# Half of image 0's convolution units placed among the attention slots of image 1

## The chip, the cores and the metric

The kernel runs on one core of a Trainium2 chip. The metric is the device time of one execution in microseconds (us). Three runs of the kernel before the change gave 2925.95, 2923.47 and 2923.46 us, median 2923.47 us.

## What is computed

The input x has 2 images of 256 channels and 64 x 64 pixels, all in float32. Two layers follow each other.

```python
# layer 0: attention over all 4096 pixels, 8 heads of 32, then a 1x1 convolution and a mask
q = proj(Wq, bq) / sqrt(32); k = proj(Wk, bk); v = proj(Wv, bv)
attn = softmax(einsum('bnd,bmd->bnm', q, k))
fuse = einsum('bnm,bmd->bnd', attn, v)
x = conv1x1(concat([x, fuse]), Wf, bf) * m + x * (1 - m)
# layer 1: channel gate, attention in 8x8 windows (4 heads of 64), shuffle, grouped convolutions
x = x * sigmoid(relu(xp @ ca_w1 + ca_b1) @ ca_w2 + ca_b2)
x = x + window_attention(x)
x = x.reshape(b, 4, 64, h, w).transpose(0, 2, 1, 3, 4).reshape(b, c, h, w)
y = relu(bn1(conv7x7(x, sa_w1, groups=64)))          # 4 channels in, 1 out per group
y = bn2(conv7x7(y, sa_w2, groups=64))                # 1 in, 4 out per group
return x * sigmoid(y)
```

## The kernel before the change

A prologue computes q, k and v of both images and writes them to DRAM. Then follows the function `pipeline`, in three stretches.

**Slots.** The attention of layer 0 is 1024 slots `(b, c, g, m)`: image b, chunk c of 512 query pixels (8 per image), group g of 4 heads (2), block m of 128 keys (32). One chunk is 64 slots. A slot has the matmuls of `scores` (L633, tile `sa`, array cut into pieces of 32 rows by 64 columns), three `Exp` activations from PSUM on ACT (L646, tile `ea`), the matmuls of `products` (L669, tile `ava`, pieces of 128 rows by 32 columns) and an addition of 128x2048 on DVE (L675). Scores are issued two slots ahead of products. The PSUM banks of the scores come from two pools: three single banks, of which a slot takes two, and two pairs, of which it takes one. They are handed out in turn, so a bank is free again when ACT has read what stood in it.

**Stages.** What follows the attention of a chunk is the generator `stage`: the 1x1 convolution (`hya`), the channel gate (`ca1a`, `ca2a`), the window attention (`qka`, `sca`, `vwa`, `pta`, `oa`) and the output projection (`opa`). One step of it is issued after every fourth slot of the next chunk. Its last step writes the rows of layer 1's x to the DRAM tensor `xs` (L989) for the convolutions. The generator `bands` fills the convolutions' banded weights in DRAM (`ws`), one DMA after every fifth slot.

**Convolutions.** The 64 groups are worked off in 16 units of 4 groups. A unit of an image is: weights `wa` (896 KB, L1029) and rows (420 KB, `xea` or `xla`, L1036) loaded over SP's queue; `conv1` (L1057, `c1a`, pieces of 128x32); a `Relu` on ACT (L1065); `conv2` (L1082, `c2a`, pieces of 32x64); two `Tanh` (L1093) and a `Copy` (L1099) on ACT; the gate on DVE (L1110); 12 stores to the output (L1128, L1130). All of it runs at the end. The generator `convolve` takes the items of the list below in turn; each of its steps issues `conv1` of item k+1 and then `conv2` of item k. The first eight items need only image 0's rows and are issued between the stages of the last chunk. From the ninth on, an item needs rows that the last stage writes. In this text an item is named by its number, from 0: `c1(8)` is `conv1` of the ninth item.

```python
items = [(u, (0,)) for u in range(EARLY)] + [(u, (1,)) for u in range(2, EARLY)]
items += [(u, (0, 1)) for u in range(EARLY, NU)] + [(1, (1,)), (0, (1,))]
```

So items 0 to 13 are units of one image, items 14 to 21 work on both images at once, and items 22 and 23 are of one image again. Each engine runs its instructions in program order. Stores that are to go over ACT's queue are kept in `held` and issued after the next item's `conv2`, behind ACT's work on it.

Of the kernel before, what the change touches and what calls it, by code (L numbers as in the profile page):

```python
# [10 lines left out]
F32 = mybir.dt.float32  # L11
# [8 lines left out]
P = 128  # L20
# [12 lines left out]
EARLY = 8  # L33
# [17 lines left out]
ROOM = 4 * len(BLOCKS) * UG * WP  # L51
# [6 lines left out]
def conv_seq_kernel(ctx: ExitStack, tc: tile.TileContext, a, out):  # L58
# [464 lines left out]
    def pipeline(arm, shifted, pools):  # L523
# [130 lines left out]
        def products(i):  # L654
            b, c, g, m = slots[i]
            chains = 1 if (b, c) == (B - 1, NCHUNK - 1) else 2
            if m == 0:
                acc[0] = avp.tile([P, CH], F32, tag="av", name=f"av{arm}_{i}")
                acc[1] = ep.tile([P, HG, CH], F32, tag="sum", name=f"sum{arm}_{i}", bufs=3)
                totals[b, c, g] = acc[1]  # L660
                if chains == 2:
                    room = cpool.tile([P, ROOM], F32, tag="room", name=f"odd{arm}_{i}")
                    acc[2] = room[:, 0 : HG * CH].rearrange("p (h n) -> p h n", h=HG)
# [67 lines left out]
        def stage(b, c):  # L731
# [241 lines left out]
            for oc in range(KC):  # L973
# [5 lines left out]
                for n, (x0, _, _) in enumerate(BLOCKS):  # L979
# [4 lines left out]
                    for h in range(2):  # L984
                        q = 2 * oc + h
                        p = 32 * q + 1 - x0

                        eng = nc.sync if h == 1 and (b, c) == (B - 1, NCHUNK - 1) else nc.gpsimd
                        eng.dma_start(  # L989
                            x_s[b, n, p + r0 : p + r1].rearrange("r g w -> g r w"),  # L990
                            xo[64 * h : 64 * h + 64, oc, r0 - WS * c : r1 - WS * c, :],
                        )
# [5 lines left out]
        items = [(u, (0,)) for u in range(EARLY)] + [(u, (1,)) for u in range(2, EARLY)]  # L998
        items += [(u, (0, 1)) for u in range(EARLY, NU)] + [(1, (1,)), (0, (1,))]
        staged, held = [], deque()  # L1000

        def convolve():
            nb = len(BLOCKS)


            early, xcs, ycs = [], [], []
            room = cpool.tile([P, ROOM], F32, tag="room", name=f"xe{arm}")
            room = room.rearrange("p (k n g w) -> p k n g w", k=4, n=nb, g=UG)
            for k in range(4):
                early.append(room[:, k])  # L1010
            for k in range(2):
                t = cpool.tile([P, B * nb, WP], F32, name=f"yc{arm}{k}")
                nc.gpsimd.memset(t, 0.0)
                ycs.append(t)
            xs, ws, ys = {}, {}, {}

            weights = deque([*range(1, NU), 1])
            dst = out.rearrange("b (g i) r w -> b i r g w", i=4)

            def load_w(u):  # L1020
                if u >= NU:
                    return
                n = 2 * 32 * UW
                if u == 0:
                    t = cpool.tile([P, n], F32, name=f"w{arm}{u}")
# [6 lines left out]
            def load_x(k):  # L1032
                u, images = items[k]
                x = xs[k] = early[k % 4] if k < EARLY else xcs[k % 4]
                for i, b in enumerate(images):
                    nc.sync.dma_start(  # L1036
                        x[:, nb * i : nb * i + nb].rearrange("p n g w -> p n (g w)"),
                        x_s[b, :, :, UG * u : UG * u + UG, :].rearrange("n p g w -> p n (g w)"),
                    )

            def load_rows(k):

                while len(xs) < min(k + 1, len(items)) and (
                    staged or B - 1 not in items[len(xs)][1]
                ):
                    load_x(len(xs))

            def conv1(k):
                if k >= len(items):
                    return  # L1050
                u, images = items[k]
                n = nb * len(images)
                w = ws[u][:, 0 : 32 * UW].rearrange("p (m g d) -> p g d m", g=UG, d=KS)
                s = psum1(f"c1{arm}{k}")
                for d in range(KS):
                    for j in range(4):
                        nc.tensor.matmul(  # L1057
                            s[32 * j : 32 * j + 32, 0 : n * W],
                            w[:, j, d, :],
                            xs[k][:, 0:n, j, d : d + W],  # L1060
                            start=(d == 0),
                            stop=(d == KS - 1),
                        )
                y = ys[k] = ycs[k % 2]
                nc.scalar.activation(  # L1065
                    y[:, 0:n, PAD : PAD + W],
                    s[:, 0 : n * W].rearrange("p (n x) -> p n x", x=W),
                    AF.Relu,
                    bias=cbias1[:, u : u + 1],
                )  # L1070

            def conv2(k):
                u, images = items[k]
                n = nb * len(images)
                y = ys.pop(k)
                w = ws[u][:, 32 * UW :].rearrange("p (m d) -> p d m", d=KS)
                tiles = [psum2(f"c2{arm}{k}_{hh}") for hh in range(2)]
                for d in range(KS):
                    for j in range(4):
                        r = slice(32 * j, 32 * j + 32)  # L1080
                        for o in HALVES:
                            nc.tensor.matmul(  # L1082
                                tiles[j // 2][o, j % 2, 0 : n * W],
                                w[r, d, o],
                                y[r, 0:n, d : d + W],
                                start=(d == 0),
                                stop=(d == KS - 1),
                            )
                zs = []
                for m in range(len(images)):  # L1090
                    z = pool.tile([P, 4, nb * W], F32, tag="z", name=f"z{arm}{k}_{m}", bufs=4)
                    for hh in range(2):
                        nc.scalar.activation(  # L1093
                            z[:, 2 * hh : 2 * hh + 2, :],
                            tiles[hh][:, :, m * nb * W : (m + 1) * nb * W],
                            AF.Tanh,
                            scale=0.5,
                        )
                    nc.scalar.activation(z, z, AF.Copy, bias=0.25, scale=0.25)  # L1099
                    zs.append(z.rearrange("p j (n x) -> p j n x", x=W))  # L1100
                while held:
                    held.popleft()()
                return zs

            def gate(k, zs):
                u, images = items[k]
                for m, b in enumerate(images):
                    z = zs[m]
                    x = xs[k][:, nb * m : nb * m + nb, :, PAD : PAD + W]
                    nc.vector.tensor_mul(z, z, x.rearrange("p n g x -> p g n x"))  # L1110

                    engines = (nc.gpsimd, nc.sync)
                    if k >= len(items) - 2:
                        engines = (nc.scalar, nc.sync)
                    elif staged and k < EARLY:
                        engines = (nc.gpsimd, nc.scalar)
                    stores = 0
                    for n, (x0, r0, r1) in enumerate(BLOCKS):
                        for i in range(4):
                            p = 32 * i + 1 - x0  # L1120
                            stores += 1
                            args = (
                                dst[b, i, r0:r1, UG * u : UG * u + UG, :],
                                z[p + r0 : p + r1, :, n, :],
                            )
                            eng = engines[stores % len(engines)]
                            if eng is nc.scalar:
                                held.append(lambda a=args: nc.scalar.dma_start(*a))  # L1128
                            else:
                                eng.dma_start(*args)  # L1130
                if k == len(items) - 1:
                    while held:
                        held.popleft()()


            def more():
                if staged and not xcs:

                    for n in range(3):
                        t = ep.tile([P, HG, CH], F32, tag="sum", name=f"xl{arm}{n}", bufs=3)  # L1140
                        t = t.rearrange("p h n -> p (h n)")[:, 0 : B * nb * UG * WP]
                        xcs.append(t.rearrange("p (n g w) -> p n g w", n=B * nb, g=UG, w=WP))
                    xcs.append(pool.tile([P, B * nb, UG, WP], F32, name=f"xl{arm}3"))
                    load_rows(EARLY + 3)
                return bool(xcs)


            load_rows(3)
            load_w(0)
            pool = yield  # L1150
            for _ in range(4):
                load_w(weights.popleft())
            conv1(0)
            yield
            for k, (u, images) in enumerate(items):
# [167 lines left out]
```

## Time and profile before

| what | value |
|---|---|
| median of three runs | 2923.47 us |
| the profiled execution | 2921.04 us |
| its span, first to last instruction | 2919.3 us |
| PE busy with matmuls | 2881.9 us, 99% of the span |
| ACT busy | 2455.9 us, 84% |
| DVE busy | 2434.9 us, 83% |
| POOL busy | 315.1 us, 11% |
| granted TensorE clock, mean | 0.996 |
| last product of the attention begins | about 2700.4 us |
| last matmul ends | about 2904.8 us |

The span is counted from the first instruction. PE is TensorE's matmuls, PEld its weight loads, ACT ScalarE, DVE VectorE, POOL GpSimd, SP the engine whose queue issues most DMAs. A row of a timeline gives the start, the duration of the merged group, the engine, the line of the kernel, the tile written and read, and the idle time of the engine before it with what ended it. The profiler records every matmul of the program as two instructions. The profiled execution is 2.4 us below the median of the runs; differences that are worked out from it are added to the median.

### The profile page before, as it was taken

The numbers are of one execution on the slowest core, as the hardware profiler recorded it, in microseconds if no ns is written. First come the engines' busy times: TensorE is split into PE (matmuls) and PEld (weight loads), VectorE is DVE, ScalarE is ACT, GpSimd is POOL, SyncE is SP. The second block draws the span as 40 slices with busy tenths as digits, with TensorE's granted clock in tenths as the row PEclk, the third lists the DMA queues.
The fourth block names the chain that finished last, engine by engine and source line by source line (L and its number), as shares of the span: only waits on it lengthen the run. The fifth ranks groups of instructions, "written<-read, shape, count | busy, mean of one in ns | idle before, by whom it ended". The sixth has DMA issues, their size and how long they took to land.

```text
span 2919.3 us, 85528 instructions
## 1 busy us (share of the span) xinstructions
PE 2881.9 (99%) x37322; PEld 837.2 (29%) x37322; DVE 2434.9 (83%) x1356; ACT 2455.9 (84%) x4143; POOL 315.1 (11%) x560
## 2 busy tenths in 40 slices
PE   9999999999999999999999999999999999999998
PEld 3551222222222222222222222222222222222665
DVE  3339999899999898998989999989899899999211
ACT  5569989898989898988989898989899898989433
POOL 8010000000000101010000000000101010000356
PEclk9999999999999999999999999999999999999999
DMA  8545422222232323242222223222324232232474
GB/s 245 202 172 174 134 75 63 78 68 80 56 88 65 90 61 91 65 80 71 70 75 69 79 55 82 64 83 63 77 73 84 70 73 75 69 113 88 117 228 120
DMA packets 231124, 276.26 MB, mean 95 GB/s; under 512 B 118672, under 2 KB 135252, under 8 KB 230484
## 3 DMA queue, kind: packets, MB, share of 16 engines
q1 hardware_dynamic: 200996, 231.74, 27.3%
q0 software_dynamic: 22416, 35.61, 5.5%
q8 instruction: 295, 4.83, 0.7%
q10 hardware_dynamic: 7328, 3.36, 0.4%
q14 instruction: 89, 0.73, 0.1%
HBM read 221.88 MB, written 66.39 MB: 99 GB/s over the span
## 4 chain that ended last, share of the span: by engine, by line
PE 97%; DMA 1%; ACT 1%; DVE 0%; issue 0%; SPq 0%; POOL 0%; ACTq 0%; DVEq 0%; POOLq 0%
PE sa L633 37%; PE ava L669 35%; PE hya L519 4%; PE qka L519 4%; PE c2a L1082 2%; PE q L428 2%; PE c1a L1057 2%; PE opa L519 2%; PE vwa L519 2%; PE v L465 2%; PE k L428 2%; PE dna L695 1%; PE sca L847 1%; PE pta L922 1%; PE oa L941 1%; PE ca2a L785 1%
## 5 line engine op out<-in xcount | busy, mean ns | idle before, releaser
L646 ACT ACTIVATE ea<-sa 128x512 f32<-128x512 f32 (+1 forms) x3072 | 2036.7, 746 | 51.6 <-PE sa L633 26.6
L633 PE MATMUL sa<-qa,ka 32*64 32x512 f32 x16384 | 1145.9, 613 | 1.5 <-ACT vst L473 1.2
L675 DVE TENSOR_TENSOR suma<-suma,ea 128x2048 f32<-128x2048 f32 x480 | 1097.4, 2286 | 5.7 <-ACT ea L646 0.5
L669 PE MATMUL ava<-ea,va 128*32 128x512 f32 x8192 | 1091.1, 605 | 1.0
L675 DVE TENSOR_TENSOR odda<-odda,ea 128x2048 f32<-128x2048 f32 x420 | 959.4, 2284 | 50.6 <-ACT ea L646 50.6
L633 PEld LDWEIGHTS sa<-qa,ka 32*64 32x64 f32 x16384 | 241.7, 129 | 785.4 <-ACT ea L646 713.6
L669 PEld LDWEIGHTS ava<-ea,va 128*32 128x32 f32 x8192 | 161.5, 108 | 834.1 <-issue 804.6
L989 POOL DMA_DIRECT2D xs<-xo x94 | 66.6, 716 | 1761.8 <-DVE xo L974 1758.8
L675 DVE TENSOR_TENSOR suma<-ea,ea 128x2048 f32<-128x2048 f32 x32 | 73.2, 2287 | 58.8 <-ACT ea L646 58.8
L519 PE MATMUL qka<-ua,qkv_w 128*32 128x512 f32 x1024 | 115.8, 592 | 0.3 <-DVE ua L803 0.3
L1130 POOL DMA_DIRECT2D out_dram<-za x180 | 101.3, 571 | 77.8 <-DVE za L1110 56.3
L447 DVE TENSOR_REDUCE top<-sq 128x512 f32<-128x2048 f32 x16 | 36.6, 2286 | 81.6 <-ACT sq L441 81.6
L750 ACT ACTIVATE ta<-hya,bf 128x512 f32<-128x512 f32 x32 | 20.2, 683 | 97.3 <-PE hya L519 91.3
L1110 DVE TENSOR_TENSOR za<-za,xla 128x768 f32<-128x768 f32 x24 | 23.0, 960 | 94.3 <-ACT za L1099 53.7
L707 POOL DMA_DIRECT2D invs<-inva x62 | 34.1, 558 | 599.2 <-DVE inva L721 438.9
L754 DVE TENSOR_TENSOR ta<-ta,mca 128x512 f32<-128x512 f32 x32 | 22.0, 688 | 77.4 <-ACT ta L750 77.4
L868 ACT ACTIVATE ewa<-ewa,mxwa 128x64 f32<-128x64 f32 x256 | 85.3, 346 | 1.5 <-DVE mxwa L859 1.5
L1082 PE MATMUL c2a<-yca,wa 32*64 32x192 f32 (+1 forms) x2688 | 83.7, 387 | 2.6 <-issue 2.3
L1093 ACT ACTIVATE za<-c2a 128x384 f32<-128x384 f32 x64 | 27.8, 486 | 57.9 <-PE c2a L1082 41.6
L826 ACT ACTIVATE qka<-qka,qkv_b 128x512 f32<-128x512 f32 x64 | 40.3, 681 | 40.8 <-PE qka L519 40.8
L1082 PEld LDWEIGHTS c2a<-yca,wa 32*64 32x64 f32 x2688 | 64.7, 192 | 22.0 <-issue 12.7
L677 DVE TENSOR_TENSOR suma<-suma,odda 128x2048 f32<-128x2048 f32 x30 | 68.8, 2292 | 1.0
(138 smaller groups left out, 1675.9 us busy)
## 6 DMA issues: line engine op xcount, KB each, us to landing
ka<-ks SPq DMA_DIRECT2D x256, 256.0 KB
va<-vs SPq DMA_DIRECT2D x256, 256.0 KB
wa<-ws SPq DMA_DIRECT2D x17, 896.0 KB
ws<-zeros SPq DMA_DIRECT2D x16, 896.0 KB
xs<-xo POOLq DMA_DIRECT2D x78, 140.0 KB, 6.0
xla<-xs SPq DMA_DIRECT2D x24, 420.0 KB
x<-in_x_dram SPq DMA_DIRECT2D x16, 512.0 KB
qs<-qst SPq DMA_DIRECT2D x16, 512.0 KB
```

What stands on the lines that cost most here:

```text
L428: nc.tensor.matmul(s[:, g, :], w[:, kc, g * P : (g + 1) * P], rhs, start=(kc == 0), stop=(kc == KC - 1),)
L465: nc.tensor.matmul(sv[:, m, :], xs0[i][:, kc, m * P : (m + 1) * P], wv[:, kc, :], start=(kc == 0), stop=(kc == KC - 1),)
L519: nc.tensor.matmul(out[o : o + 32], weights[:, o : o + 32], x, start=start, stop=stop)
L633: nc.tensor.matmul(heads[j][o], k[r, cols][:, o], q[r, g, :], start=True, stop=not shifted)
L646: nc.scalar.activation(e[:, h, :], tile, AF.Exp, scale=SCALE0)
L669: nc.tensor.matmul(av[r, :], v[:, m % PB, r], e[:, j, :], start=start, stop=stop)
L675: nc.vector.tensor_add(total, first.pop(m % chains, total), e)
L677: nc.vector.tensor_add(acc[1], acc[1], acc[2])
L868: nc.scalar.activation(e[:, n, :], e[:, n, :], AF.Exp, bias=mx[:, n : n + 1], accum_out=rs[:, n : n + 1],)
L989: eng.dma_start(x_s[b, n, p + r0 : p + r1].rearrange("r g w -> g r w"), xo[64 * h : 64 * h + 64, oc, r0 - WS * c : r1 - WS * c, :],)
L1082: nc.tensor.matmul(tiles[j // 2][o, j % 2, 0 : n * W], w[r, d, o], y[r, 0:n, d : d + W], start=(d == 0), stop=(d == KS - 1),)
L1130: eng.dma_start(*args)
```

## The change

Units 0 to 7 of image 0 leave the end. A new generator `quiet` works them off among the slots of image 1 from its chunk 1 on, one step after every eighth slot, so two units in a chunk and all eight in chunks 1 to 4. Its four steps are: load weights and rows; `conv1`; `conv2` with its activations; gate and stores (all 12 over POOL's queue). The rest, 24 items, are all of one image: units 8 to 15 of image 0, units 8 to 15 of image 1, units 0 to 7 of image 1, in this order. For it:

- `bands` takes a step after every third slot, so that the weights are in DRAM before the first quiet unit.
- Weights are loaded 24 times instead of 17; rows that the last stage writes are loaded one item at a time, up to six items ahead, into six buffers (four, for two images each, before).
- In the last stage the rows written to `xs` go over ACT's and SP's queues instead of POOL's and SP's.
- The last item is evicted, gated and stored in three blocks of columns; the last three items' stores go over ACT and SP.

```diff
-EARLY = 8
+QUIET = 8
...
-                        eng = nc.sync if h == 1 and (b, c) == (B - 1, NCHUNK - 1) else nc.gpsimd
+                        eng = nc.gpsimd
+                        if (b, c) == (B - 1, NCHUNK - 1):
+                            eng = (nc.scalar, nc.sync)[h]
...
-        items = [(u, (0,)) for u in range(EARLY)] + [(u, (1,)) for u in range(2, EARLY)]
-        items += [(u, (0, 1)) for u in range(EARLY, NU)] + [(1, (1,)), (0, (1,))]
+        items = [(u, 0) for u in range(QUIET, NU)] + [(u, 1) for u in range(QUIET, NU)]
+        items += [(u, 1) for u in range(QUIET)]
+        fill = NU - QUIET
...
+        def evict(z, parts, cols):
+            for tile, h in parts:
+                nc.scalar.activation(z[:, h, cols], tile, AF.Tanh, scale=0.5)
+            nc.scalar.activation(z[:, :, cols], z[:, :, cols], AF.Copy, bias=0.25, scale=0.25)
...
+        def quiet():
+            for u in range(QUIET):
+                w = cpool.tile([P, 2 * 32 * UW], F32, tag="w0", name=f"wq{arm}{u}")
+                nc.sync.dma_start(w, w_s[u])
+                x = rows_of(cpool.tile([P, XU], F32, tag="xq", name=f"xq{arm}{u}"))
+                load_rows_of(x, u, 0)
+                yield
+                conv1(f"q{arm}{u}", u, w, x, ycs[u % 2])
+                yield
+                one, pair = psum1(f"c2q{arm}{u}_0"), psum2(f"c2q{arm}{u}_1")
+                last = psum1(f"c2q{arm}{u}_2")
+                conv2(w, ycs[u % 2], (one, pair[:, 0, :], pair[:, 1, :], last))
+                z = cpool.tile([P, 4, nb * W], F32, tag="zq", name=f"zq{arm}{u}")
+                parts = ((one, 0), (pair, slice(1, 3)), (last, 3))
+                parts = [(t[..., 0 : nb * W], h) for t, h in parts]
+                evict(z, parts, slice(0, nb * W))
+                yield
+                gate(z, x, slice(0, nb))
+                for n in range(nb):
+                    store(u, 0, n, z, (nc.gpsimd,))
+                yield
...
             def more():
                 if staged and not xcs:
...
+                        xcs.extend(rows_of(t[:, XU * k : XU * k + XU]) for k in range(2))
+                if unit[0] + 3 < fill:
+                    load_rows(unit[0] + 3)
+                elif xcs:
+                    load_rows(min(len(xs), unit[0] + 5))
                 return bool(xcs)
...
+            def finish(k, z, out_of):
+                u, b = items[k]
+                if k == len(items) - 1:
+                    for n in range(nb):
+                        out_of(slice(W * n, W * n + W))
+                        gate(z, xs[k], slice(n, n + 1))
+                        store(u, b, n, z, (nc.sync, nc.scalar))
+                    flush()
+                    return
+                gate(z, xs[k], slice(0, nb))
+                engines = (nc.gpsimd, nc.sync)
+                if staged and k < fill:
+                    engines = (nc.gpsimd, nc.scalar)
+                elif k >= len(items) - 3:
+                    engines = (nc.scalar, nc.sync)
+                for n in range(nb):
+                    store(u, b, n, z, engines)
...
-            if i % 5 == 1:
+            if i % 3 == 1:
                 next(banded, None)
+            if i % 8 == 2 and b == B - 1 and c > 0:
+                next(hushed, None)
```

## The prediction

> **What bounds the kernel now.** First the page: who is busy, and what the chain that ended last is made of.
>
> ```profile
> PE   9999999999999999999999999999999999999998
> ...
> ACT  5569989898989898988989898989899898989433
> ...
> PE 97%; DMA 1%; ACT 1%; DVE 0%; issue 0%; SPq 0%; POOL 0%; ACTq 0%; DVEq 0%; POOLq 0%
> ```
>
> PE carries the chain, but ACT is nearly as full among the slots and half empty at the end. Whether a slot has room for a convolution is therefore read from PE's timeline, where a stage's block stands between slots:
>
> ```profile
> 1149.29 1.11 PE L633 MATMUL sa<-qa,ka 32*64 32x512 f32 x16
> ...
> 1151.22 3.62 PE L519 MATMUL hya<-xa,WfT 128*32 128x512 f32 x32
> 1154.66 3.62 PE L519 MATMUL hya<-fa,WfT 128*32 128x512 f32 x32
> 1158.20 1.11 PE L633 MATMUL sa<-qa,ka 32*64 32x512 f32 x16
> ...
> 1160.24 1.11 PE L633 MATMUL sa<-qa,ka 32*64 32x512 f32 x16
> ...
> 1164.32 1.11 PE L633 MATMUL sa<-qa,ka 32*64 32x512 f32 x16
> ...
> 1166.25 1.05 PE L519 MATMUL ca1a<-x1a,ca_w 128*32 128x256 f32 x16
> 1167.23 1.11 PE L633 MATMUL sa<-qa,ka 32*64 32x512 f32 x16
> ```
>
> Scores start every 2.04 us. With the block `hya` the interval is 8.91 us: all of the block's 6.87 us is added. ACT's timeline for the same moment:
>
> ```profile
> 1158.34 1.26 ACT L750 ACTIVATE ta<-hya,bf 128x512 f32<-128x512 f32 x2 [5.92 <-PE hya L519]
> 1159.49 7.95 ACT L646 ACTIVATE ea<-sa 128x512 f32<-128x512 f32 x12
> ```
>
> ACT sat idle for 5.92 us, so every score bank was free, and PE could have run ahead. It did not: the next interval is 2.04 again (1158.20 to 1160.24). So 2.04 us is PE's own pace. ACT needs 7.95 us for four slots, 1.99 us for one: it is just fast enough, with little to spare.
>
> Last, PE's timeline of the end, and under it one stretch of the end (length; busy time of PE, PEld, DVE, ACT, POOL; clock, DMA share, GB/s):
>
> ```profile
> 2772.76 3.76 PE L1082 MATMUL c2a<-yca,wa 32*64 32x192 f32 x107 [1.73 <-issue]
> 2780.61 4.26 PE L1057 MATMUL c1a<-xla,wa 128*32 128x192 f32 x56 [4.09 <-ACT yca L1065]
> 2784.80 2.64 PE L1082 MATMUL c2a<-yca,wa 32*64 32x192 f32 x112
> 2787.37 2.53 PE L1057 MATMUL c1a<-xla,wa 128*32 128x192 f32 x56
> 2789.83 2.64 PE L1082 MATMUL c2a<-yca,wa 32*64 32x192 f32 x112
> ```
>
> ```profile
> 2775.00:2780.00 5.00, 1.52 (x35) 0.88 (x20) 0.00 (x0) 0.00 (x0) 0.57 (x1) 0.50 1.07 359
> ```
>
> The convolutions too are PE-bound: 2.46 us from `c2a` to the next `c1a` ending (2787.37 to 2789.83), 2.57 us for `c2a` (2784.80 to 2787.37). Items of two images take 4.73 and 4.80 us (chain of waits, 2822.69 on). The one real hole is at 2771 to 2781, where item 8 waits for rows that the last stage writes; the clock falls to 0.50 in it.
>
> **Added among the slots.** Eight `conv1` and eight `conv2`. The end's price is 2.46 + 2.57 = 5.03 us a unit. From below: `ca1a`, in `conv1`'s array form and beside slots, adds 2.90 - 2.04 = 0.86 us (1164.32 to 1167.23) for 16 matmuls of 256 columns. Scaled, 56 of 192 columns give 0.86 x 56/16 x 192/256 = 2.25 us; the two-image items agree (4.73 - 2.46 = 2.27). `conv2` likewise is between 4.80 - 2.57 = 2.23 and 2.57. What lies between the ends is a change of array form. In the slots `conv1` follows products of its own form and `conv2` comes before scores of its own form, so I take 2.3 + 2.4 = 4.7 us, near the lower end; eight units: 37.6 us (36 to 40.3).
>
> ACT adds per unit a `Relu` of 0.42, two `Tanh` reads and a `Copy`, 1.73 us in the end's rows (0.87 for two `Tanh` reads, 0.85 the `Copy`; here three reads, hence some 0.1 more). While PE is in the block ACT would have idled, but the eviction can only begin when `conv2` is over, and queued behind it on ACT are the next slot's exponentials, for which PE's scores two slots on wait. The nearest row is a copy of `f` (0.59 us on ACT) followed by one of `ewa` (0.6 us, beside 0.62 us on PE): the score interval behind them is 2.32, a stall of 0.28 us. I take 0.4 us a unit, 3.2 in all (0, as behind `hya`, to 1.0 each). Together **+40.8 us** (36 to 48).
>
> At nothing: DVE's gate (0.96 us) and POOL's 12 stores (12 x 0.57 = 6.8 us), in steps at slots 26 and 58 of a chunk, away from the stage's own stores at slots 0 and 8. SP gets two loads (896 and 420 KB) every 32 slots; queued behind them are key and value loads, asked for eight slots (16 us) ahead. A weight load took 6.1 us in the busy end (chain of waits, 2798.39), so the cover holds; without it up to 6 us for each of eight loads. `bands` issues the same DMAs in three fifths of the time: during the 16 fills of `ws` the DMA share is some 0.45 over 10 us stretches, and it would be some 0.75; PE's intervals show no trace of these fills now. Zero, with 2 us kept for the range.
>
> A rule speaks for more room: the Trainium skill, Perfetto Trace Analysis, "Identifying the Most-Contended Engine", says that PE's matmul occupancy does not tell how near it is to its limit, and names weight loads' busy share (here 29%) instead. By it the slots would have room and only ACT's 2.2 us a unit would be paid, some 18 us instead of 40.8; the 2.04 us behind an idle ACT says that the room cannot be used by this order of instructions.
>
> **Taken from the end.** Up to `conv1` of item 8 the list has the same eight items of one image, so PE's order is the same there. From 2780.61 to the last matmul's end at 2904.80 were 124.2 us: eight `c1a` of one image (19.7), eight of two (37.8), nine `c2a` of one (23.1), eight of two (38.4), sum 119.0, and 5.2 of waits and slow clock (`c1a` at 2780.61 took 4.26 for 2.46). After: 16 x 2.46 + 17 x 2.57 = 83.1 us. Of the eight moved units, worth 40.2 us, 4.4 is given back, because 8 x 9.53 for pairs become 16 x 5.03. Waits after: slow clock 1.8 again, 0.3 before the last `conv2` (2902.43), and for the DMA 1.5. The last is the unknown: in items 9 to 15 each unit loads weights and rows and stores, 0.92 + 0.43 + 0.26 MB in 5.03 us, 320 GB/s, where the trace moved some 300 at a full DMA share. Loads are asked for five items ahead and buffers are six, so data are not late; instructions may be (the "issue" idle of 0.55 us at 2811.46, in a like stretch of 13 us). By that rate 35 us cost 1.5 us; 0 to 6. So 86.7 against 124.2: **-37.5 us** (-39 to -32).
>
> **The hole.** The rows of item 8 were asked for at 2772.76, when POOL's second store of `xs` (issued 2765.64) had landed at 2772.5, as the waits for `xs` have it. On ACT's queue that store would go out beside SP's. SP's loads then start perhaps 1 to 2 us earlier. `c1a` itself waits for `yca`, which stands on ACT behind six held stores, the last issued at 2779.77 while SP's loads ran; that stays. I take **-1.5 us** (+1, ACT's two new issues in the way, to -5.8, the whole idle time).
>
> The Trainium skill, DMA: Bandwidth & Descriptors, "Issuing engines are not separate DMA queues", says that another issuing engine saves only issue time. The issues are alike (0.7 us on POOL, 0.69 on SP), so by it this term would be about 0.
>
> **The drain.** 14.5 us from the last matmul to the end. After: ACT has 12 held stores (some 0.42 each, 5 us) before the last eviction, which in three blocks is nearer 2.9 than 1.7 us; six stores instead of twelve follow. Gain and loss nearly cancel: **-0.5** (-3 to +2).
>
> Sum: 40.8 - 37.5 - 1.5 - 0.5 = **+1.3 us**, span 2920.6; on the median 2923.47 + 1.3, rounded, **2925.0 us**. It is moved work, not removed work: PE is full where it leaves and full where it arrives.
>
> **The rivals.** *ACT becomes the bound among the slots (slower).* ACT's 1.99 of 2.04 us leaves no cover, and each unit's 0.42 + 1.8 us is paid on top of PE's block, less the 0.4 counted: 8 x 1.8 = 14.6 us, 2939; with half of it 2932. For it: its 89 to 99% busy slices. Against: in the `hya` block it caught up 5.92 us. It decides from 0.6 us more stall per unit than I count.
>
> *The full DMA starves the end (slower).* If the waits of 2809 to 2815 (0.55 and 1.16 us) return with each of seven units, 7 x 1.7 = 12 less 1.5: 2935. For it the 320 GB/s, against it the five items of lead.
>
> *The hole closes (faster).* `xs` lands early, the idle 4.09 + 1.73 us and the slow clock's 1.8 go, and the blocks save 1.5 us of drain: 1.3 - (5.8 - 1.5) - 1.8 - 1.0 = -5.8; with no ACT stall (-3.2) -9: 2914 to 2918. Against it: the held stores on ACT.
>
> *It doesn't do what it says:* the slots hide the units after all; +18 instead of +40.8 gives 2902. The 2.04 behind `hya` nearly excludes it.
>
> **How the numbers follow.** Forecast case, near zero: 0.42, its own range 2918 to 2930. ACT rival 0.19, DMA rival 0.14, closed hole 0.22, hidden 0.03. About 0.2% (5.8 us) is what a measurement of this kernel can tell from no change. So faster 0.25, same 0.42, slower 0.33. The range reaches to the lower end of the closed hole with the units at 36 us, 2912, and to 2937, between the DMA and the ACT rival.
>
> **What would show it.** Among the slots with quiet steps, score intervals near 4.3 and 4.5 to 4.8 us; a chunk of 168 to 170 us instead of 158.8 in four chunks, and unchanged others. Intervals of 4.1 for both would show hidden work; over 5.5 behind `conv2`, ACT. At the end `c1a` and `c2a` in a period of 5.03 us, 24 units; the wait before item 8 a little under 4 us. Wrong if the first row of the last part starts well before 2776 (moved by the slots' delay), or if gaps of over 0.5 us stand in each of items 9 to 15.

## The result and the profile after

The changed kernel took 2939.79 us (median of five runs, 2936.98 to 2945.31); the kernel before took 2924.54 us beside it (five runs). The ratio is 1.0056, with a 95% interval of 1.0042 to 1.0071: slower by 15 us, where I had forecast 2925.0 and no measurable change. The profiled execution took 2939.65 us, its span is 2937.9 us. Three marks cut the span into the terms of the prediction: the start of the attention's last product, the start of `c1(8)`, and the end of PE's last matmul.

| stretch | before, us | after, us | difference | forecast |
|---|---|---|---|---|
| start to last product | 2700.4 | 2742.7 | +42.3 | +40.8 |
| last product to `c1(8)` | 80.2 | 83.1 | +2.9 | -1.5 |
| `c1(8)` to PE's end | 124.4 | 96.8 | -27.6 | -37.5 |
| PE's end to the end | 14.3 | 15.4 | +1.1 | -0.5 |
| span | 2919.3 | 2937.9 | +18.6 | +1.3 |

The page first: ACT's busy slices, the instruction queue (packets, MB, share of the DMA engines), and the chain that ended last.

```profile
ACT  5569989898989898989989898989889898989533
...
q8 instruction: 305, 5.00, 0.7%
...
PE 96%; DMA 1%; ACT 1%; issue 1%; DVE 0%; ACTq 0%; POOL 0%; SPq 0%; POOLq 0%; DVEq 0%
```

PE still carries the chain, but 1% of it is now "issue", time in which an engine waited for nothing that the profile shows; before it was 0%. The `q8` line matters further down: 5.00 MB in 305 packets are 16 KB each. The page counts 38666 matmuls of PE and as many weight loads, 77332 instructions or some 254 for each packet, so `q8` is taken to be the queue of PE's instructions.

Among the slots, PE's timeline around a quiet `conv1`:

```profile
1613.66 1.11 PE L633 MATMUL sa<-qa,ka 32*64 32x512 f32 x16
1614.70 1.07 PE L668 MATMUL ava<-ea,va 128*32 128x512 f32 x8
1615.59 2.48 PE L1025 MATMUL c1qa<-xqa,wqa 128*32 128x192 f32 x56
1618.00 1.11 PE L633 MATMUL sa<-qa,ka 32*64 32x512 f32 x16
```

and the timeline of PE and ACT around a quiet `conv2`:

```profile
1639.14 1.11 PE L633 MATMUL sa<-qa,ka 32*64 32x512 f32 x16
...
1641.18 2.71 PE L1045 MATMUL c2qa<-yca,wqa 32*64 32x192 f32 x112
...
1643.59 1.67 PE L633 MATMUL sa<-qa,ka 32*64 32x512 f32 x16
1643.80 0.94 ACT L1055 ACTIVATE zqa<-c2qa 128x192 f32<-128x192 f32 x3 [1.49 <-PE c2qa L1045]
1644.76 0.85 ACT L1056 ACTIVATE zqa<-zqa 128x768 f32<-128x768 f32 x1
...
1646.18 1.11 PE L633 MATMUL sa<-qa,ka 32*64 32x512 f32 x16
```

The score intervals are 4.34 us (1613.66 to 1618.00, so +2.30), 4.45 (+2.41) and behind it 2.59 (+0.55): 5.26 us a unit. A chunk with two units lasts 169.3 us (1587.36 to 1756.64) instead of 158.8, four times.

The end, PE's timeline from `c1(8)` on:

```profile
2815.51 2.80 PE L1045 MATMUL c2a<-yca,wa 32*64 32x192 f32 x112
2825.77 4.45 PE L1025 MATMUL c1a<-xla,wa 128*32 128x192 f32 x56 [7.45 <-ACT yca L1032]
2830.15 2.64 PE L1045 MATMUL c2a<-yca,wa 32*64 32x192 f32 x112
2832.72 2.55 PE L1025 MATMUL c1a<-xla,wa 128*32 128x192 f32 x56
2835.20 2.64 PE L1045 MATMUL c2a<-yca,wa 32*64 32x192 f32 x112
...
2867.54 2.65 PE L1045 MATMUL c2a<-yca,wa 32*64 32x192 f32 x112
2870.11 0.88 PE L1025 MATMUL c1a<-xla,wa 128*32 128x192 f32 x12
2871.91 2.19 PE L1025 MATMUL c1a<-xla,wa 128*32 128x192 f32 x44 [0.92 <-issue]
2874.03 2.24 PE L1045 MATMUL c2a<-yca,wa 32*64 32x192 f32 x84
2878.40 0.96 PE L1045 MATMUL c2a<-yca,wa 32*64 32x192 f32 x28 [2.12 <-issue]
...
2886.81 0.59 PE L1045 MATMUL c2a<-yca,wa 32*64 32x192 f32 x3
2888.84 2.61 PE L1045 MATMUL c2a<-yca,wa 32*64 32x192 f32 x109 [1.43 <-issue]
2891.38 1.20 PE L1025 MATMUL c1a<-xla,wa 128*32 128x192 f32 x19
2894.06 1.88 PE L1025 MATMUL c1a<-xla,wa 128*32 128x192 f32 x37 [1.49 <-issue]
```

Up to 2850 a unit takes 5.05 us (2830.15 to 2835.20), as forecast. Then waits stand in the middle of a `c1a` or `c2a`, which no semaphore explains: 0.52, 0.50, 0.92, 2.12, 1.43 and 1.49 us between 2853 and 2894, 7.0 in all. Their places are regular: 44 + 84 = 128 recorded matmuls stand between the waits of 0.92 and 2.12 us, 109 + 19 = 128 between those of 1.43 and 1.49, and 255 between the other neighbours. With as many weight loads that is 256 or 510 instructions, so the waits stand one or two packets of `q8` apart. A wait costs more than its idle time: the two `c2a` around the wait of 0.92 start 6.49 us apart (2867.54 to 2874.03), 1.46 more than 5.03. The eight units from the `c2a` at 2850.30 to the one at 2901.14 take 50.8 us instead of 40.2: 10.6 us for the waits.

### The profile page after: what moved, and what is told of

Read it like the earlier page. It is cut to its first block, busy times and chain, and to the rows that moved or that the text cites. A ratio compares the mean times of both kernels' runs of the same rounds, so it can differ in the third digit from the quotient of the medians.

```text
span 2937.9 us, 88143 instructions
## 1 busy us (share of the span) xinstructions
PE 2892.5 (98%) x38666; PEld 868.6 (30%) x38666; DVE 2436.1 (83%) x1358; ACT 2458.2 (84%) x4165; POOL 336.7 (11%) x600
## 4 chain that ended last, share of the span: by engine, by line
PE 96%; DMA 1%; ACT 1%; issue 1%; DVE 0%; ACTq 0%; POOL 0%; SPq 0%; POOLq 0%; DVEq 0%
PE sa L633 37%; PE ava L668 35%; PE hya L519 4%; PE qka L519 4%; PE vwa L519 2%; PE opa L519 2%; PE c2a L1045 2%; PE v L465 2%; PE c1a L1025 2%; PE q L428 2%; PE k L428 2%; PE dna L694 1%; PE c2qa L1045 1%; PE sca L846 1%; PE c1qa L1025 1%; PE oa L940 1%
## 5 line engine op out<-in xcount | busy, mean ns | idle before, releaser
L1074 POOL DMA_DIRECT2D out_dram<-zqa x96 | 53.8, 568 | 487.6 <-ACT ea L646 293.2
L1060 DVE TENSOR_TENSOR za<-za,xla 128x768 f32<-128x768 f32 (+1 forms) x18 | 15.7, 871 | 80.3 <-DMA out_dram<-za 44.1
L1074 POOL DMA_DIRECT2D out_dram<-za x126 | 71.0, 571 | 82.3 <-DVE za L1060 53.4
L1045 PE MATMUL c2a<-yca,wa 32*64 32x192 f32 x2688 | 67.0, 331 | 5.3 <-issue 4.9
L674 DVE TENSOR_TENSOR odda<-ea,ea 128x2048 f32<-128x2048 f32 x30 | 68.5, 2284 | 0.2 <-ACT ea L646 0.2
```

The source lines that it names most:

```text
L674: nc.vector.tensor_add(total, first.pop(m % chains, total), e)
L1045: nc.tensor.matmul(banks[j][o, 0 : nb * W], w[r, d, o], y[r, :, d : d + W], start=(d == 0), stop=(d == KS - 1),)
```

## Experiments

Theory F: PE's instructions come late in the last part because the weight loads fill the DMA there. Its rival D: they come late because units of one image use up instructions twice as fast as pairs, whatever the DMA does. Theory H, for the wait before `c1(8)`: ACT cannot run the `Relu` because it stands behind held stores; its rival: the rows are late. Each kernel was timed in three rounds beside the kernel before, whose medians there were 2924.2 to 2924.7 us.

**The price among the slots** (`a_noquiet`): the changed kernel without the quiet units; units 0 to 7 of image 0 are not computed.

```diff
-                for _ in hushed:
-                    pass
...
-            if i % 8 == 2 and b == B - 1 and c > 0:
-                next(hushed, None)
```

> The changed kernel without the eight quiet units: units 0 to 7 of image 0 are not computed at all, the rest of the program is the same. Theory (moved work is paid in full among the slots): four chunks of 169.3 us go back to 158.8, and the span falls by 42 us to about 2896, the last part staying as it is. Rival 1 (the slots hide part of it): falls by 20 to 36 us. Rival 2 (the quiet units also spoil what follows, by their loads or their buffers): falls by more than 45 us, with a shorter last part.

Measured: 2892.76 us, ratio 0.9891 [0.9871, 0.9911], 47.0 less than with the units (47.4 between the profiled executions). The last product starts at 2699.86, 42.8 us earlier. The units are paid in full where they were put. The other 4.6 us of the 47.4 are from the end, 3.0 of them before `c1(8)`: this is what the second rival said, that the quiet units also cost something after them.

**The stall behind a quiet `conv2`** (`a_copy`): the quiet units' `Copy` moves from ACT to DVE, and into the next step, eight slots later.

```diff
-                evict(z, parts, slice(0, nb * W))
+                for tile, h in parts:
+                    nc.scalar.activation(z[:, h, :], tile, AF.Tanh, scale=0.5)
                 yield
+                nc.vector.tensor_scalar_mul(z, z, 0.25)
+                nc.vector.tensor_scalar_add(z, z, 0.25)
```

> The changed kernel with the Copy of the quiet units (x 0.25 + 0.25) on DVE in two steps instead of ACT. If the next scores wait because ACT comes back late from the eviction (0.55 us a unit now, of 5.25), the interval behind conv2's falls from 2.59 to 2.1 to 2.3, a chunk with two quiet units from 169.3 to about 168.5, and the time by 2 to 4 us to about 2936 to 2938. If the wait is PE's own (a change of array form, or the scores' banks), nothing moves, or DVE's products come later and it is slower.

Measured: 2939.45 us, ratio 1.0057 [1.0039, 1.0075], no change. Its timeline at the same place:

```profile
1643.47 1.67 PE L633 MATMUL sa<-qa,ka 32*64 32x512 f32 x16
1643.68 0.94 ACT L1096 ACTIVATE zqa<-c2qa 128x192 f32<-128x192 f32 x3 [1.48 <-PE c2qa L1045]
1644.54 2.00 ACT L646 ACTIVATE ea<-sa 128x512 f32<-128x512 f32 x3
```

The exponentials begin 1 us earlier than in the changed kernel, and the scores behind `conv2` still take 1.67 us instead of 1.11. So my reason for the 0.4 us, exponentials queued behind the eviction, is wrong; that the size was near was luck. What remains is that the scores need banks that `conv2` has just filled and that the three `Tanh` must read first (0.94 us); that was not tried by itself.

**The instruction waits.** `a_spread` moves the seven weight loads of items 9 to 15 to seven items up to 19:

```diff
-                if k < 4 or k > fill:
+                if k < 4 or k in (9, 11, 13, 14, 16, 17, 19):
                     load_w()
```

> The changed kernel, with the seven weight loads of the last part spread over items 9 to 19 (after items 9, 11, 13, 14, 16, 17, 19) instead of one after each of items 9 to 15. Nothing else differs. Theory F (instruction blocks come late because data loads fill the DMA): the 7.0 us in which PE waits for nothing but its own sequencer inside items 13 to 18 fall to 2 or less, and the time falls by 4 to 6 us against the changed kernel, to a span near 2933. Rival D (units of one image need twice the instructions per microsecond, whatever the DMA does): the waits stay at 6 to 8 us, span 2937 to 2939.

Measured: 2939.43 us, ratio 1.0052 [1.0036, 1.0069]; PE's idle time after `c1(8)` 6.0 us (7.3 in the changed kernel), later and smaller; one wait of 1.22 us is now for weights. No gain in time. By what I had expected this spoke for D. But the three large waits (1.34, 1.05 and 1.13 us) again follow late packets on `q8`, and in the 2 us before each of these began (at 2880.40, 2889.30 and 2894.72) the DMA share was 0.98, 1.01 and 1.03: there the DMA was still full.

`a_split` cuts each of these loads in four pieces, one behind each step:

```diff
-                nc.sync.dma_start(t, w_s[u])
+                for r in range(0, P, 32):
+                    pieces.append((t[r : r + 32], w_s[u, r : r + 32]))
```

> The changed kernel with each of the seven weight loads of items 9 to 15 cut into four loads of 32 partitions, one behind each step of an item (3 per item, so over items 9 to 18). Same bytes, no burst of 0.92 MB. If an instruction block is late because it stands behind a burst (theory F1), PE's idle time after item 8 falls from 7.3 us to under 4 and the time to 2935 to 2937. If it is late in proportion to the bytes that go past it (theory F2), the idle time stays at 6 to 8 us, spread further, and the time at 2938 to 2941.

Measured: 2941.74 us, ratio 1.0053 [1.0036, 1.0070]; idle time 5.6 us. Not the burst of a single load, then.

`a_nold` leaves the loads out; units 0 to 7 of image 1 use the weights of units 8 to 15:

```diff
+                if u < QUIET and QUIET + u in ws:
+                    ws[u] = ws[QUIET + u]
+                    return
```

> The last part of the changed kernel without its second round of weight loads: units 0 to 7 of image 1 use the weights of units 8 to 15, which are still in place (other outputs, same instructions on PE). This takes 7 x 0.92 = 6.4 MB out of the DMA between about 2840 and 2890; rows and stores stay, some 140 GB/s in place of 320. If PE's instructions come late because the transfers fill the DMA (theory F), the idle time of PE after item 8 falls from 7.3 us to about the 2.0 of the kernel before, and the time from 2939.8 to about 2935. If they come late because units of one image use up instructions faster (theory D: 336 instructions in 5.03 us, where a pair of images uses 336 in 9.53), the idle time stays at 5 to 8 us and the time within 1.5 us of 2939.8.

Measured: 2933.42 us (2928.70 to 2936.60, all runs below all of the changed kernel's), ratio 1.0029 [1.0016, 1.0042]. `c1(8)` to PE's end is 89.5 us instead of 96.8, with 1.6 us idle. Windows of 10 us (length; busy time of PE, PEld, DVE, ACT, POOL with counts; clock, DMA share, GB/s), the changed kernel:

```profile
2850.00:2860.00 10.00, 9.48 (x316) 8.05 (x312) 1.63 (x2) 3.48 (x8) 6.74 (x12) 1.00 0.93 264
2860.00:2870.00 10.00, 9.50 (x320) 8.17 (x310) 1.92 (x2) 3.39 (x6) 5.18 (x10) 1.00 0.90 266
2870.00:2880.00 10.00, 6.96 (x195) 5.67 (x188) 0.96 (x1) 2.77 (x6) 4.93 (x9) 1.00 0.92 274
```

and `a_nold`, which in this stretch is at the same items within one:

```profile
2850.00:2860.00 10.00, 10.00 (x350) 8.89 (x344) 1.92 (x2) 4.28 (x8) 6.71 (x13) 1.00 0.59 147
2860.00:2870.00 10.00, 10.00 (x345) 8.89 (x340) 1.92 (x2) 4.30 (x8) 6.66 (x13) 1.00 0.52 120
2870.00:2880.00 10.00, 10.00 (x338) 8.92 (x330) 1.92 (x2) 4.29 (x8) 6.50 (x13) 1.00 0.59 143
```

PE's instructions are the same in both; at a DMA share of 0.9 PE does 195 to 320 matmuls in 10 us, at 0.55 some 345. D alone falls, F holds: it is the bytes, not their grouping.

`b_load` asks the other way round: the kernel before, with one more load of 0.92 MB behind each of items 8 to 14.

```diff
+                if EARLY <= k < EARLY + 7:
+                    t = ep.tile([P, HG, CH], F32, tag="e", name=f"wx{arm}{k}")
+                    t = t.rearrange("p h n -> p (h n)")[:, 0 : 2 * 32 * UW]
+                    nc.sync.dma_start(t, w_s[k])
```

> The kernel before, with one more load of 0.92 MB (weights that nobody reads) behind each of items 8 to 14. PE's instructions are the same, at 336 in 9.53 us. DMA rises there from some 240 to some 330 GB/s for about 65 us. Theory F: PE's idle time after item 8 rises from 2.0 us by 3 to 7 us, without a DMA named as the releaser, and the time to 2927 to 2931. Theory D: idle time 2.0 to 3.0 us, time within 1.5 us of the kernel before. A third outcome, waits that end with a load of rows or weights, would say that the extra loads made data late, and would tell nothing of instructions.

Measured: 2937.97 us, ratio 1.0049 [1.0032, 1.0066]. It is the third outcome: 8.0 us of PE's waits among the pairs end with a load of rows. It still says one thing. PE's timeline and the windows where the pairs have begun:

```profile
2832.43 4.81 PE L1057 MATMUL c1a<-xla,wa 128*32 128x384 f32 x56 [1.36 <-DMA xla<-xs]
2837.17 4.87 PE L1082 MATMUL c2a<-yca,wa 32*64 32x384 f32 x112
2841.97 4.83 PE L1057 MATMUL c1a<-xla,wa 128*32 128x384 f32 x56
```

```profile
2830.00:2840.00 10.00, 8.64 (x184) 5.54 (x176) 0.96 (x1) 2.31 (x4) 3.38 (x6) 1.00 0.95 325
2840.00:2850.00 10.00, 10.00 (x192) 5.91 (x184) 1.92 (x2) 3.90 (x7) 4.89 (x9) 1.00 0.93 315
```

At a share of 0.93 to 0.95 no wait named "issue" stands among the pairs (184 to 192 matmuls in 10 us); the only one after `c1(8)`, 2.60 us at 2807.57, stands among units of one image. By this the waits need both: a full DMA and instructions used up at the one-image rate, and D would be half of the cause. This half is not shown: the waits for rows also gave PE's instructions time to catch up.

**The hole before `c1(8)`.** `a_xs` puts the last stores of `xs` back on POOL and SP:

```diff
-                        if (b, c) == (B - 1, NCHUNK - 1):
-                            eng = (nc.scalar, nc.sync)[h]
+                        eng = nc.sync if h == 1 and (b, c) == (B - 1, NCHUNK - 1) else nc.gpsimd
```

> The changed kernel with the last two stores of xs on POOL and SP, as before, instead of ACT and SP. The forecast gave this edit -1.5 us. If ACT's queue brought the rows earlier, xs lands later here, the loads of item 8 are issued 0.5 to 2 us later after the last product and the time is 2940 to 2942. If the end of the hole is set by ACT behind its held stores in any case, the time before item 8 stays at 82 to 84 us after the last product and the time within 1 us of 2939.8.

Measured: 2941.74 us, ratio 1.0053 [1.0036, 1.0069]; last product to `c1(8)` 83.4 us against 83.1. ACT's queue for `xs` is worth nothing here. The two us of the median are in the last part (9.5 us idle). `a_pool` takes the stores of items 4 to 7 from ACT:

```diff
-                    engines = (nc.gpsimd, nc.scalar)
+                    engines = (nc.gpsimd,)
```

> The changed kernel, with the stores of items 4 to 7 all on POOL's queue, so that none are held on ACT. Theory H (the hole before item 8 lasts until ACT gets past its held stores, whose issue waits while SP's row loads are expanded): the Relu of item 7 runs early, item 8 starts when its rows land, 3 to 4 us after SP asks for them; the idle 7.45 us before it shrink to 2 to 3.5 us, the time falls by 4 to 5 us. Rival R (the rows land late anyway, behind the five other row loads asked for together): idle stays over 6 us, time within 1 us.

Measured: 2934.70 us, ratio 1.0032 [1.0019, 1.0044]. ACT's timeline in the changed kernel, and then the row of `c1(8)` in `a_pool`:

```profile
2817.20 8.05 ACTq L1072 DMA_DIRECT2D out_dram<-za  x6
2825.29 0.42 ACT L1032 ACTIVATE yca<-c1a,cbias 128x192 f32<-128x192 f32 x1 [10.41 <-DMA out_dram<-za]
```

```profile
2820.47 4.71 PE L1025 MATMUL c1a<-xla,wa 128*32 128x192 f32 x56 [3.70 <-DMA xla<-xs]
```

Six stores hold ACT for 8.05 us while the first rows are loaded (the next six took 2.60), and the `Relu` stands behind them. Without them the wait falls from 7.45 to 3.70 us, and the rows are late next. H holds for the first half of the wait.

**The drain** (`a_drain`): the stores of items 21 and 22 go over POOL and SP instead of ACT and SP.

```diff
-                elif k >= len(items) - 3:
-                    engines = (nc.scalar, nc.sync)
```

> The changed kernel, with the stores of items 21 and 22 on POOL and SP as those of earlier items, so that ACT has no held stores in front of the last item's eviction. Theory (the drain of 15.5 us is long because ACT issues 12 stores before it evicts the last item): the eviction begins with the last matmul's end instead of 6 us later, the drain falls to 9.5 to 11 us, the time by 4.5 to 6 us. Rival (the drain is set by the landing of the last stores on SP's queue and the DMA): within 1.5 us of the changed kernel.

Measured: 2939.91 us, ratio 1.0051 [1.0033, 1.0069]. In the changed kernel ACT issued 12 held stores before the last eviction:

```profile
2919.87 8.34 ACTq L1072 DMA_DIRECT2D out_dram<-za  x12
...
2928.57 0.45 ACT L1055 ACTIVATE za<-c2a 128x128 f32<-128x128 f32 x2 [7.91 <-DMA out_dram<-za]
```

In `a_drain` the last eviction follows `conv2` at once, and the drain falls from 15.4 to 13.6 us, 1.8 us of the 4.5 to 6 that I had expected; what fills the rest of it was not tried. The last part had 9.5 us of idle PE instead of 7.3, which hid the gain: the waits vary by some us from one kernel to the next.

**The kernel before, mended.** Three kernels apply this to the kernel before. `b_pool` makes `a_pool`'s edit there (the stores of items 4 to 7 over POOL alone):

> The kernel before with the stores of items 4 to 7 on POOL alone instead of POOL and ACT. If the Relu of item 8 stands on ACT behind six held stores (theory H), the idle time before item 8 falls from 5.8 us to 2 to 4 and the time to 2920 to 2922; if it waits for the rows of the last stage, nothing moves: 2923 to 2925. Instruction waits after it can take up to 2 us back.

Measured: 2920.02 us (10 runs), ratio 0.9981 [0.9972, 0.9991]: faster than both. Last product to `c1(8)` is 75.7 us instead of 80.2; the last part gives 2.1 back. What the edit takes off ACT is, in the kernel before:

```profile
2769.01 11.08 ACTq L1128 DMA_DIRECT2D out_dram<-za  x6
```

`b_best` keeps this, adds two items of image 0 ahead of the hole, and spreads the last item's stores over three queues:

```diff
-EARLY = 8
+EARLY = 10
...
-                    if k >= len(items) - 2:
-                        engines = (nc.scalar, nc.sync)
+                    if k == len(items) - 1:
+                        engines = (nc.scalar, nc.sync, nc.gpsimd)
```

> The kernel before (no quiet units) with the first stores of its last part on POOL alone, two more items of image 0 ahead of item 8 (ten instead of eight), and the last item's stores over ACT, SP and POOL. If the hole at item 8 is a wait for the last rows and for ACT behind its held stores, two more items of 5.03 us of work fit into it: the idle 5.8 us falls under 1.5, and what a pair saves over two units of one image (0.53 us each) is paid twice. Expected: 2913 to 2918, against 2923.5. If stores on POOL or instruction waits take it back: 2920 to 2926.

Measured: 2929.84 us, ratio 1.0016 [1.0006, 1.0025], a miss. The hole closed: `c1(10)`, the first item that now needs the last stage's rows, starts without a wait. But from `c1(8)` on PE idled for 12.1 us, nearly all of it "issue", with more units of one image beside the weight loads. `b_early2` keeps the ten items, leaves the last item's stores as they were and spreads the loads over twice the time:

```diff
-                if weights and (weights[0] <= 1 + EB or k >= EARLY):
+                if weights and (weights[0] <= 1 + EB or k in (11, 13, 15, 17, 18, 19, 20)):
```

> The kernel before with stores of items 4 to 7 on POOL alone, ten items of image 0 ahead of the hole, and the weights of the pairs loaded behind items 11, 13, 15, 17, 18, 19, 20 instead of one behind each item from 10 on (seven loads over 62 us instead of 31). b_best (10 items too, loads not spread) had 12.1 us of idle PE in its last part, 9.7 of them instruction waits. If those come from the loads that run beside units of one image, they fall to 3 to 5 us and the time to 2917 to 2922, under the kernel before; if not, it stays at 2926 to 2931.

Measured: 2923.71 us, ratio 0.9994 [0.9984, 1.0004], idle time 8.5 us: 6 us better than `b_best`, and no better than the kernel before. Here, unlike in `a_spread`, five of the seven loads went out after the first pair's `conv1` had begun (from 2840.20 on, against 2837.53), which is what the reading of `b_load` asks for.

## Why the prediction was wrong

*The slots: right.* 42.3 us against 40.8. `conv1` and `conv2` cost 2.30 and 2.41 (2.3 and 2.4 forecast), the stall 0.55 (0.4, for another reason than I gave). Nothing was hidden, ACT did not become the bound.

*The last part: the term that failed.* The work was right: 5.05 us a unit wherever PE did not wait. The step "35 us cost 1.5 us; 0 to 6" was mis-sized; the waits measured 10.6 us, which is 9.1 of the 9.9 us by which the stretch was missed. The rows of the kernel before that the step was scaled from are

```profile
2811.46 2.29 PE L1082 MATMUL c2a<-yca,wa 32*64 32x192 f32 x94 [0.55 <-issue]
2814.91 5.10 PE L1057 MATMUL c1a<-xla,wa 128*32 128x384 f32 x56 [1.16 <-DMA out_dram<-za]
```

I scaled the one wait of 0.55 us in 13 us, in a stretch where the DMA had only just become full (share 0.97 to 1.00 from 2800 on) and the one-image units were about to end; the second wait, 1.16 us at 2813.75, I left to the rival. In the steady state there were six waits in 41 us, 1.16 us each, and each took another 0.6 around it. The prediction's *full DMA* rival had the mechanism and nearly the time, 2935, with chance 0.14. My case against it, five items of lead, was about data; data were not late, and that protects no instruction.

The records of the packets show how. Some 256 of PE's instructions fill one 16 KB packet on `q8` (305 packets for 77332, and the waits 256 or 510 apart); at 336 instructions in 5.03 us one is used up in 3.8 us. From 2851.7 to 2891.7 nine packets began, 5.0 us apart; in `a_nold` from 2850.4 to 2891.0 eleven, 4.1 us apart. Each of the six waits ends 1.3 to 2.0 us after a packet has come in. A packet takes about 1 us in both kernels, so what is late is its start; why the full DMA delays the start is not shown. The Trainium skill, Runtime: NRT & Kernel Launch, "Instruction fetch mechanics", says that an engine's own DMA queue fetches the next block of 256 instructions while the present one runs, and that crossing a block's end is mostly hidden. The packets agree with the first; against the second stand waits of 0.50 to 2.12 us.

*The hole: wrong.* Forecast -1.5 for `xs` over ACT; `a_xs` shows 0.3, so nothing. The Trainium skill's rule that the prediction set against this term (DMA: Bandwidth & Descriptors, "Issuing engines are not separate DMA queues"), by which it would be about 0, was the better guide. The +2.9 us of the stretch stand elsewhere, in the last stage, where PE's row of `hya` reads

```profile
2761.72 5.22 PE L519 MATMUL hya<-fa,WfT 128*32 128x512 f32 x32 [2.84 <-DVE fa L726]
```

and in the kernel before

```profile
2718.33 3.64 PE L519 MATMUL hya<-fa,WfT 128*32 128x512 f32 x32 [1.68 <-DVE fa L727]
```

That is 1.2 us more wait and 1.6 us of slow clock behind it (the granted clock is 0.75 from 2763 to 2767, and 1.00 in the kernel before). The wait is 2.4 to 3.1 us in all but one of the kernels with quiet units (0.87 in `a_copy`) and 1.4 to 1.7 in those without. The DVE step that it ends with waits for the load of `rda`. SP issues this load 4.60 us after the store of `invs` that it reads, 3.04 in the kernel before; it is 4.2 to 4.7 us in every kernel with the long wait and 2.85 to 3.04 in the others, `a_copy` among them. So the load goes out late; why it does stays open.

*The drain: wrong.* I counted the 12 held stores at 0.42 us each and let them cancel against the shorter eviction. They took 8.34 us, 0.70 each, and the eviction waited for them; +1.1 instead of -0.5. Without them, in `a_drain`, the drain is 0.7 us shorter than in the kernel before.

Together: 1.5 for the slots, 9.9 for the last part, 4.4 before `c1(8)` and 1.6 for the drain are the 17.3 us between the span forecast, 2920.6, and the one measured (rounded terms). Three small slips in the working carry no weight: 16 x 5.03 less 8 x 9.53 is 4.2 us, not 4.4; 1164.32 to 1167.23 is 2.91 us, not 2.90; and PE's last matmul ends at 2905.0 by its row, not at 2904.8.

## What to carry to other kernels

Here work was moved from one place where PE was full to another. That gained nothing, and the place that it left got worse: pairs of 384 columns became units of 192, so PE used up instructions nearly twice as fast, and seven more loads of 0.9 MB filled the DMA beside them. Price a matmul-dense stretch by its instructions and by its bytes per microsecond together; a buffer lead protects data only. Ask of each store on ACT's queue what stands behind it: taking 24 stores off that queue was the only edit here that beat the kernel before (0.19%).

## What was unexpected of the hardware

PE waited for its own instructions, up to 2.12 us at a time in the changed kernel (DMA share 0.90 to 0.93 over 10 us) and 3.68 us in `b_best` (share 0.95 from 2836 to 2840); spreading or splitting the loads did not help while they ran beside units of one image. Six DMA issues took ACT 8.05 us while SP's row loads ran, and 2.60 us after them. After the 7.45 us wait the granted clock was 0.52 (2825 to 2830): `c1a` took 4.45 us instead of 2.53 to 2.55.
